# Writing the turned image from inside the chunk steps instead of between images (attention layer and selective scan, one Trainium2 core)

## The chip, the cores and the metric

The kernel runs on one core of a Trainium2 chip. A core has five engines with instruction streams of their own: TensorE (PE; its weight loads are listed apart as PEld), VectorE (DVE), ScalarE (ACT), GpSimd (POOL) and SyncE (SP), which here only issues transfers. Sixteen DMA engines move data between HBM and the on-chip memory (SBUF, 128 partitions); matrix products land in PSUM. An instruction waits for others through semaphores, and each engine takes its instructions in order. The metric is the device time of one execution in microseconds: 9565.71 us, the median of three runs of the kernel before.

## The reference

Two layers act on eight images of 128 x 128 pixels with 128 channels. Layer 0 is linear attention with a normalization. Layer 1 is a gated state-space layer with four scan directions. Cut to what matters for the change:

```python
xb, z = split(x @ Win)                      # 256 channels each
xb = silu(depthwise_conv3x3(xb) + conv_b)   # u
xf = xb.reshape(Bb, Cd, L)                  # rows first
xt = transpose(xb, (0, 1, 3, 2)).reshape(Bb, Cd, L)   # columns first: the turned image
xs = stack([xf, xf[..., ::-1], xt, xt[..., ::-1]])
x_dbl = einsum('bcl,cd->bdl', xs, Wxproj)   # 8 rows of dt, 1 of B, 1 of C
delta = softplus(dt_weight @ dt + dt_bias)
# scan: state = exp(delta*A)*state + delta*u*B ;  y = state*C + u*D
y = y0 + back(y1) + turn_back(y2) + turn_back(back(y3))
out = layernorm(y * silu(z)) @ Wout
```

The batch and the four directions are folded together in a way that mixes them: image `b` serves as direction `b // 2` for the outputs 0 to 3 (b even) or 4 to 7 (b odd). So the terms `u*D` of images 4, 6, 2 and 0 (and of 5, 7, 3 and 1) are summed into the same arrays.

## The kernel before

Three stages run one after another. `layer0` computes the attention and writes `x1` to HBM. `layer1_front` makes u from `x1` (projection, convolution, silu) and writes what the scans read: u times B in natural and in turned order (`ubs`), the ten rows of dt, B and C (`xds`, and split into three bfloat16 parts in both orders, `xps`), and the sums of u times D (`gts`, then `gs`). `layer1_scan` runs the scans and the output, behind a barrier of all engines (L722). The change lies in `layer1_front`.

**The front.** It goes through the images in the order of `SEQ` (4, 6, 5, 7, 0, 1, 2, 3). An image is 16 chunks of 1024 pixels (8 columns w of 128 h), and `step(n)` (L639) is one chunk: 128 steps, software pipelined from n-1 to n+2. Channels are two halves `c` of 128 partitions. The instruction order within each engine is exactly the program order (`in_order`).

In a step, TensorE projects (`project`, L475) and computes two of the nine convolution taps (`taps_pe`, L499). ScalarE copies the projection out of PSUM with the two edge columns that neighbouring chunks exchange (`place`, L483: L487, L491, L492), and computes three taps (`taps_act`, L513), which GpSimd adds up (L515). VectorE adds these to the PSUM sum (L521) and computes four taps (L523). ScalarE applies the silu (`silu`, L530) into `ures`, which holds the whole image. `rows` (L539) makes the ten rows, `keep_rows` (L544) stores them through two alternating buffers, `spread` (L551) spreads B over the partitions with the selector `bsel`, and `by_b` (L560) multiplies `ures` in place and stores it. `sum_d` (L579) scales u by D. Except for images 4 and 5, whose term is the first, the earlier sum is loaded (`load_sum`, L577; a gathering load, L575, for images 0 and 1), added by GpSimd (L595, or L592 for images 0 and 1) and stored again (`store_sum`, L600).

**The end of an image.** In the first step of the next image, `leave` (L626) is called in the midst of the step. It copies `ures` in turned order, in 32 pieces of 128 x 1024, into a staging buffer `turned` (L634: ScalarE for two in five, VectorE for the rest) and stores each (L635, 4096 contiguous bytes for each partition). Between them it loads the ten rows again with the columns on the partitions (L608), transposes them on TensorE (L616), splits both orders into bfloat16 parts on VectorE (`split3`, L44 and L46) and stores these (L624).

**What sets the order.** All transfers of the front are issued by SP, in program order, so a transfer whose data is late holds up all later ones. Staging buffers are rings: tag `tb` four buffers (taps, u times D, `turned`, parts), `ta`, `tc` and `d` two each. In the scan stage GpSimd issues transfers too: L855 adds `gs` onto `y` while it transfers.

Of the kernel before, what the change touches and what calls it, by code (L numbers as in the profile page):

```python
# [8 lines left out]
F32 = mybir.dt.float32  # L9
BF16 = mybir.dt.bfloat16  # L10
AF = mybir.ActivationFunctionType
# [5 lines left out]
P = 128  # L17
B = 8
# [4 lines left out]
R = 8  # L23
# [14 lines left out]
NAT, TURN = 0, 1  # L38


def split3(nc, parts, x):

    for j in range(3):
        nc.vector.tensor_copy(parts[j], x)  # L44
        if j < 2:
            nc.vector.tensor_tensor(x, x, parts[j], ALU.subtract)  # L46


def pipeline(n, stages):
# [334 lines left out]
def layer1_front(ctx: ExitStack, tc, x1, win, conv_w, conv_b, wxp, d_par, ubs, xds, xps, gts, gs):  # L384
# [25 lines left out]

    ident = const.tile([P, P], F32, name="ident1")
    make_identity(nc, ident)
    one3 = const.tile([3, P], BF16, name="one3")
    nc.vector.memset(one3, 1.0)
    cw = const.tile([P, NC2, 9], F32, name="cw")
    nc.sync.dma_start(cw, conv_w.rearrange("(c p) t -> p c t", p=P))
    cb = const.tile([P, NC2], F32, name="cb")
# [2 lines left out]
    wx = const.tile([P, NC2, 32], F32, name="wx")  # L420
    nc.vector.memset(wx, 0.0)
    nc.sync.dma_start(wx[:, :, 0 : R + 2], wxp.rearrange("(c p) r -> p c r", p=P))
    bsel = const.tile([P, 2, P], F32, name="bsel")
    for hf in range(2):
        nc.vector.tensor_copy(bsel[:, hf, :], ident[:, 32 * hf + R : 32 * hf + R + 1].to_broadcast([P, P]))
    sd = const.tile([P, K, NC2], F32, name="sd")
    nc.sync.dma_start(sd, d_par.rearrange("(k c p) o -> p k (c o)", p=P, c=NC2))
    wi = const.tile([P, NC2, P], F32, name="wi")
# [11 lines left out]
            nc.vector.tensor_tensor(wt[:, j, c, :], wi[:, c, :], p, ALU.mult)  # L440


    xins, xbs, xdt = [], [], []
    for i in range(2):
        xi = const.tile([P, CW + 1, H + 2], F32, name=f"xi{i}")
        nc.gpsimd.memset(xi, 0.0)
        xins.append(xi)
        xb = const.tile([P, NC2, CW + 2, H + 2], F32, name=f"xb{i}")
        nc.gpsimd.memset(xb, 0.0)
        xbs.append(xb)  # L450
        xd = const.tile([P, 512], F32, name=f"xd{i}")
        nc.gpsimd.memset(xd, 0.0)
        xdt.append(xd)
    ures = big.tile([P, NC2, L], F32, name="ures")
    uturn = ures.rearrange("p c (w h) -> p c h w", h=H)
    inner = slice(1, H + 1)
# [4 lines left out]
    def place_of(n):  # L461
        return SEQ[n // NCH % B], n % NCH
# [20 lines left out]
    def place(n, c):  # L483

        g = n % NCH
        xb, old = xbs[n % 2], xbs[(n - 1) % 2]
        nc.scalar.copy(xb[:, c, 1 : CW + 1, inner], pxs.pop((n, c)))  # L487
        if g == 0:
            nc.gpsimd.memset(xb[:, c, 0, :], 0.0)
        else:  # L490
            nc.scalar.copy(old[:, c, CW + 1, inner], xb[:, c, 1, inner])  # L491
            nc.scalar.copy(xb[:, c, 0, inner], old[:, c, CW, inner])  # L492
        if g == NCH - 1:
            nc.gpsimd.memset(xb[:, c, CW + 1, :], 0.0)

# [44 lines left out]

    def keep_rows(n):
        b, g = place_of(n)
        t = xdt[n % 2]
        nc.scalar.copy(t[0:64, :], prs.pop(n))  # L544
        for hf in range(2):
            s = slice(g * CH + hf * 512, g * CH + hf * 512 + 512)
            nc.sync.dma_start(xds[b][:, s], t[32 * hf : 32 * hf + R + 2, :])

    def spread(n, hf):
        pbs[n, hf] = p = pm.tile([P, 1, 512], F32, name="pb", tag="m")  # L550
        nc.tensor.matmul(p[:, 0, :], bsel[:, hf, :], xdt[n % 2], start=True, stop=True)  # L551

    def by_b(n):

# [14 lines left out]

    def load_sum(n, c):  # L570
        b, g = place_of(n)
        if b // 2 != 2:
            gls[n, c] = gl = wp.tile([P, CH], F32, name="gl", tag="d", bufs=2)
            if b // 2 == 0:
                nc.sync.dma_start(gl.rearrange("p (e q) -> p e q", e=NCH), gts[b % 2, c, :, :, g])  # L575
            else:
                nc.sync.dma_start(gl, sums_at(n, c))  # L577

    def sum_d(n):  # L579
        b, g = place_of(n)  # L580
        s = b // 2
        for c in range(NC2):
            t = wp.tile([P, CH], F32, name="du", tag="tb", bufs=4)
            u, dst = ures[:, c, g * CH : g * CH + CH], t
            if s >= 2:
                u = u.rearrange("p (w i h) -> p w i h", w=CW, h=8)
                dst = t.rearrange("p (i w h) -> p w i h", w=CW, h=8)
            nc.scalar.activation(dst, u, AF.Copy, scale=sd[:, s, c : c + 1])
            if s == 0:
                gl = gls.pop((n, c)).rearrange("p (e h) -> p h e", h=8)  # L590
                tw = t.rearrange("p (w h) -> p w h", w=CW)
                nc.gpsimd.tensor_tensor(tw, tw, gl, ALU.add)  # L592
            elif s != 2:
                gl = gls.pop((n, c))
                nc.gpsimd.tensor_tensor(gl, gl, t[:, ::-1] if s % 2 == 1 else t, ALU.add)  # L595
                t = gl
            dus[n, c] = t

    def store_sum(n, c):
        nc.sync.dma_start(sums_at(n, c), dus.pop((n, c)))  # L600

    half = (R + 2) // 2
    xws = {}

    def load_rows(b, i):
        r = slice(i * half, i * half + half)
        xws[b, i] = x = wp.tile([P, half, H], F32, name="xw", tag="d", bufs=2)
        nc.sync.dma_start(x, xds[b].rearrange("r (w h) -> w r h", h=H)[:, r, :])  # L608

    def split(b, i):  # L610

        r = slice(i * half, i * half + half)
        x = xws.pop((b, i))
        pt = pj.tile([P, half, P], F32, name="ptx", tag="pj")
        for j in range(half):
            nc.tensor.transpose(pt[:, j, :], x[:, j, :], ident)  # L616
        y = wp.tile([P, half, W], F32, name="xh", tag="tb", bufs=4)
        nc.scalar.copy(y, pt)
        for order, v in ((TURN, y), (NAT, x)):
            q = wp.tile([P, 3, half, P], BF16, name="parts", tag="tb", bufs=4)  # L620
            split3(nc, [q[:, j] for j in range(3)], v)
            dst = xps[b, order].rearrange("j r (a e) -> a j r e", e=P)
            for j in range(3):
                nc.sync.dma_start(dst[:, j, r, :], q[:, j])  # L624

    def leave(b):  # L626

        for i in range(2):
            load_rows(b, i)
        for k in range(NC2 * NCH):  # L630
            c, i = divmod(k, NCH)
            t = wp.tile([P, CW, W], F32, name="turned", tag="tc" if k % 3 == 2 else "tb", bufs=2 if k % 3 == 2 else 4)
            copy = nc.scalar.copy if k % 5 in (1, 3) else nc.vector.tensor_copy
            copy(t, uturn[:, c, i * CW : i * CW + CW, :])  # L634
            nc.sync.dma_start(ubs[b, TURN][c][:, i * CH : i * CH + CH], t.rearrange("p h w -> p (h w)"))  # L635
            if k % 10 == 9 and k < 20:
                split(b, k // 10)

    def step(n):  # L639

        live, then, later, before = 0 <= n < N, 0 <= n + 1 < N, 0 <= n + 2 < N, 1 <= n <= N
        b, g = place_of(n)
        if live:
            taps_dve(n, 0)
        if before:
            keep_rows(n - 1)
        if then:
            project(n + 1, 1)
            place(n + 1, 1)
        if live:  # L650
            taps_pe(n, 1)
        if later:
            load(n + 2)
        if before:
            for c in range(NC2):
                store_sum(n - 1, c)
        if live and g != 0:
            for c in range(NC2):
                load_sum(n, c)
        if before:  # L660
            for hf in range(2):
                spread(n - 1, hf)
        if before and g == 0:
            by_b(n - 1)
            leave(place_of(n - 1)[0])
        if live and g == 0:
            for c in range(NC2):
                load_sum(n, c)
        if then:
            taps_act(n + 1, 0)  # L670
        if live:
            silu(n, 0)
        if then:
            taps_pe(n + 1, 0)
        if later:
            project(n + 2, 0)
        if live:
            taps_dve(n, 1)
        if then:
            taps_act(n + 1, 1)  # L680
        if before and g != 0:
            by_b(n - 1)
        if live:
            silu(n, 1)
        if later:
            place(n + 2, 0)
        if live:
            rows(n)
            sum_d(n)

    with in_order(tc):
        for n in range(-2, N + 1):
            step(n)


@with_exitstack
def layer1_scan(ctx: ExitStack, tc, ubs, xps, zs, gs, dtw, dtb, a_log, gamma, beta, w_out, out):
# [36 lines left out]
    for dst, src, rows in ((wparts, dtw.rearrange("k r d -> r k d"), R), (bparts, dtb.rearrange("o (k d) -> o k d", d=D2), 1)):  # L734
        x = wp.tile([rows, K, D2], F32, name="w32", tag="sp", bufs=2)
        nc.sync.dma_start(x, src)
        q = wp.tile([rows, 3, K, D2], BF16, name="w16", tag="ub", bufs=4)
        split3(nc, [q[:, j] for j in range(3)], x)
        for j in range(3):
            if rows == 1:  # L740
                nc.sync.dma_start(dst[j : j + 1], q[:, j])
            else:
                nc.sync.dma_start(dst[j], q[:, j])
# [466 lines left out]
```

## Time and profile before

| what | value |
|---|---|
| median of three runs | 9565.71 us (9555.7 to 9566.26) |
| profiled execution: span of the core | 9556.3 us |
| front: first L521 to last copy of L634 | 2377.7 to 4825.1 us |
| one chunk step in the front (start of L521 to the same in the next step) | 15.26 us |
| start of an image to the start of the next | 304.6 to 306.9 us; 16 steps alone are 244.2 us |
| VectorE busy over the span | 8129.7 us (85%) |
| GpSimd busy over the span | 7192.2 us (75%) |

The span runs from the first to the last instruction of one profiled execution; the runs are timed apart. Its slices show all three stages at once; the front's own windows are read below. In lines of groups, the number after the count is the busy time in us, then the mean duration of one in ns, then the engine's idle time before them with what ended it. In windows, each engine has its busy time and its number of instructions, and the last columns are TensorE's granted clock, the busy share of the DMA engines and GB/s.

### The profile page before, as it was taken

Reading aid. Unit: us, or ns where it says so; the run is one execution under the profiler, and the core shown is the slowest. Engines: PE = TensorE matmul, PEld = TensorE weight load, DVE = VectorE, ACT = ScalarE, POOL = GpSimd, SP = SyncE. Lnnn points to the kernel's source line nnn. Section 1 sums busy time; section 2 is a strip of 40 time slices with the busy share of each in tenths; the row PEclk is TensorE's granted clock in tenths of the full one; section 3 lists DMA queues with packets and bytes.
Section 4 is the critical chain, followed back from the end, with each engine's and each line's share of the span. In section 5 each row is a group of like instructions: output and inputs, shape, how many; then the busy total and the mean of one; then the engine's idle time right before and its main releaser. Section 6 shows DMA issues by size and latency. Waiting matters only on the chain. (4 is left out here: it accounts for less than half of the span.)

```text
span 9556.3 us, 89734 instructions
## 1 busy us (share of the span) xinstructions
PE 6281.6 (66%) x24190; PEld 3101.4 (32%) x24352; DVE 8129.7 (85%) x8188; ACT 7202.0 (75%) x8288; POOL 7192.2 (75%) x4361
## 2 busy tenths in 40 slices
PE   8999999898977788777823544636345363543636
PEld 5556655554322233222300311404123040220403
DVE  6667765564988889888979999999999999999996
ACT  5556555567877788777878788888888888888884
POOL 3445544455665578776859999999999999999997
PEclk9999999999988899888955665757557585665857
DMA  2332233313476678987765957759487685867858
GB/s 91 135 133 81 95 133 132 133 71 140 172 266 232 229 262 247 266 263 269 243 204 165 257 174 207 240 174 269 154 228 219 186 260 165 244 190 198 245 165 212
DMA packets 1034807, 1851.21 MB, mean 194 GB/s; under 512 B 274852, under 2 KB 500772, under 8 KB 1026112
## 3 DMA queue, kind: packets, MB, share of 16 engines
q1 hardware_dynamic: 999488, 1711.23, 54.2%
q0 software_dynamic: 34816, 134.23, 7.3%
q8 instruction: 199, 3.26, 0.1%
q14 instruction: 304, 2.49, 0.1%
HBM read 1153.03 MB, written 692.12 MB: 193 GB/s over the span
## 5 line engine op out<-in xcount | busy, mean ns | idle before, releaser
L893 POOL TENSOR_TENSOR ubt<-ubt,sp 128x1024 f32<-128x1024 f32 x1024 | 2457.9, 2458 | 161.0 <-ACT sp L886 74.3
L882 PE MATMUL px<-rows,dtw 128*128 128x512 bf16 x1893 | 909.5, 573 | 2271.7 <-DVE y L943 1063.5
L515 POOL TENSOR_TENSOR tap<-tap 128x1024 f32<-128x1024 f32 x512 | 1206.1, 2367 | 640.1 <-ACT tap L513 517.9
L523 DVE SCALAR_TENSOR_TENSOR acc<-xb,cw,acc 128x1024 f32<-128x1024 f32 x1024 | 1320.6, 1290 | 52.7 <-ACT tap L513 0.9
L886 ACT ACTIVATE sp<-px 128x1024 f32<-128x1024 f32 x1024 | 1046.0, 1024 | 420.7 <-PE px L882 265.6
L951 POOL TENSOR_TENSOR y<-y,ubt 128x512 f32<-128x512 f32 x768 | 1160.0, 1557 | 142.9 <-DVE ubt L924 141.9
L505 PE MATMUL acc<-xi,wt 128*128 128x512 f32 x2048 | 952.2, 608 | 383.9 <-ACT ures L530 383.6
L903 DVE TENSOR_TENSOR_SCAN ubt<-px,ubt 128x1024 f32<-128x1024 f32 x512 | 1177.0, 2332 | 25.9 <-POOL ubt L893 19.2
L901 DVE TENSOR_TENSOR_SCAN ubt<-px,ubt 128x1024 f32<-128x1024 f32 x512 | 1178.3, 2332 | 14.1 <-POOL ubt L893 6.3
L882 PEld LDWEIGHTS <-dtw 128*128 128x128 bf16 x2048 | 163.9, 109 | 3066.2 <-issue 865.9
L890 ACT ACTIVATE px<-sp,sa 128x1024 f32<-128x1024 f32 x1024 | 1110.2, 1109 | 6.1
L513 ACT ACTIVATE tap<-xb,cw 128x1024 f32<-128x1024 f32 x768 | 834.0, 1139 | 68.1 <-POOL tap L515 67.8
L282 POOL TENSOR_TENSOR q<-q,qs 128x512 f32<-128x512 f32 x256 | 271.2, 1060 | 691.5 <-DVE qs L281 691.5
L886 ACT ACT_TABLE_LOAD x512 | 656.9, 1283 | 164.5 <-PE px L882 129.2
L505 PEld LDWEIGHTS acc<-xi,wt 128*128 128x128 f32 x2048 | 383.6, 192 | 928.3 <-ACT ures L530 486.1
L890 ACT ACT_TABLE_LOAD x512 | 656.9, 1283 | 9.2
L1016 PEld LDWEIGHTS px<-wg,z 128*128 128x128 f32 x4096 | 553.8, 218 | 118.6 <-issue 113.5
L909 PE MATMUL pc<-rows,csel 128*128 128x512 bf16 x1017 | 512.7, 585 | 88.9 <-DVE rstd L1004 79.9
L1016 PE MATMUL px<-wg,z 128*128 128x128 f32 x4096 | 554.1, 301 | 0.0
L478 PE MATMUL pxb<-xi,wi 128*128 128x512 f32 x1024 | 495.9, 606 | 4.3 <-ACT xb L487 4.3
L943 DVE TENSOR_TENSOR y<-y,px 128x1024 f32<-128x1024 f32 x384 | 468.7, 1221 | 14.7 <-DVE px L931 0.5
L298 ACT ACTIVATE sq<-o 128x512 f32<-128x512 f32 x256 | 161.2, 630 | 418.2 <-DVE o L296 416.9
(155 smaller groups left out, 15187.7 us busy)
## 6 DMA issues: line engine op xcount, KB each, us to landing
ubt<-ubs SPq DMA_DIRECT2D x512, 1024.0 KB
zs<-z SPq DMA_DIRECT2D x512, 256.0 KB
ubs<-ures SPq DMA_DIRECT2D x256, 512.0 KB
ubs<-turned SPq DMA_DIRECT2D x256, 512.0 KB
z<-zs SPq DMA_DIRECT2D x256, 512.0 KB
y<-gs POOLq DMA_DIRECT2D x128, 1024.0 KB, 10.5
rows<-xps SPq DMA_DIRECT2D x1536, 60.0 KB
xi<-x SPq DMA_DIRECT2D x120, 576.0 KB
```

What stands on the lines that cost most here:

```text
L505: nc.tensor.matmul(acc[:, s, :], wt[:, j, c, :], x, start=(j == 0), stop=(j == len(ON_PE) - 1))
L513: nc.scalar.activation(t, at(n, c, *d), AF.Copy, scale=cw[:, c, tap(*d) : tap(*d) + 1])
L515: nc.gpsimd.tensor_tensor(sums[n, c], sums[n, c], t, ALU.add)
L523: nc.vector.scalar_tensor_tensor(acc, at(n, c, *d), cw[:, c, tap(*d) : tap(*d) + 1], acc, ALU.mult, ALU.add)
L882: nc.tensor.matmul(p[:, hf * 512 : hf * 512 + 512], sl.dw[:, c * P : c * P + P], src, start=True, stop=True)
L886: nc.scalar.activation(t, da[n, c], AF.Softplus)
L890: nc.scalar.activation(da[n, c], sp[n, c], AF.Exp, scale=sa[:, sl.s, c : c + 1])
L893: nc.gpsimd.tensor_tensor(ubt[n][:, c, :], ubt[n][:, c, :], sp.pop((n, c)), ALU.mult)
L901: nc.vector.tensor_tensor_scan(e[:, ::-1], x[:, ::-1], e[:, ::-1], start, ALU.mult, ALU.add)
L903: nc.vector.tensor_tensor_scan(e, x, e, start, ALU.mult, ALU.add)
L951: nc.gpsimd.tensor_tensor(v[:, c], v[:, c], h[:, c], ALU.add)
L1016: nc.tensor.matmul(po[:, w, :], z[:, c, w * H : w * H + H], wg[:, c, :], start=(c == 0), stop=(c == NC2 - 1))
```

## The change

- `leave` goes. The turned copies stay 32 for each image, but each now covers 16 rows h by 64 columns w of a half image, and two are made in each step (`turn`), eight steps behind: one after the first four taps of VectorE, one at the end of the step. `copy_on` names the engine: both on GpSimd in the steps of images 4 and 5; VectorE and GpSimd in those of 6, 7, 2 and 3; VectorE and ScalarE in those of 0 and 1. That is 96 on VectorE, 113 on GpSimd, 32 on ScalarE. The last 15 are made after the last step (`tail`).
- Each copy is stored in runs of 64 elements (256 bytes) at a pitch of 512 bytes (`store_turned`), where it was 4096 contiguous bytes before.
- The rows' split is cut into five pieces of two rows, spread over ten steps of the next image (`split_step`), on VectorE in the steps of images 0 and 1, else on GpSimd. The last image's is done in `tail`.
- For images 6, 7, 2 and 3 the earlier sum is no longer loaded and added: ScalarE writes u times D (reversed) into the ring `d`, and GpSimd issues a transfer that adds it onto the sum in HBM (`add_sum`).
- `place` makes one edge copy of two columns instead of two copies. The row buffer `xd` is single instead of double, and `bsel` is replaced by a broadcast column of the identity.

```diff
@@ layer1_front
-    one3 = const.tile([3, P], BF16, name="one3")
-    nc.vector.memset(one3, 1.0)
-    bsel = const.tile([P, 2, P], F32, name="bsel")
-    for hf in range(2):
-        nc.vector.tensor_copy(bsel[:, hf, :], ident[:, 32 * hf + R : 32 * hf + R + 1].to_broadcast([P, P]))
...
+    both = const.tile([P, NC2, 2, CW + 2, H + 2], F32, name="xb")
...
+    edges = [
+        (edge[:, :, 2 * CW + 3 :: -(2 * CW + 3), 1 : H + 1], edge[:, :, 1 : 2 * CW + 3 : 2 * CW + 1, 1 : H + 1]),
+        (edge[:, :, CW + 1 : CW + 3, 1 : H + 1], edge[:, :, CW + 3 : CW - 1 : -3, 1 : H + 1]),
+    ]
@@ place
-            nc.scalar.copy(old[:, c, CW + 1, inner], xb[:, c, 1, inner])
-            nc.scalar.copy(xb[:, c, 0, inner], old[:, c, CW, inner])
+            dst, src = edges[n % 2]
+            nc.scalar.copy(dst[:, c], src[:, c])
@@ sum_d
-            elif s != 2:
-                gl = gls.pop((n, c))
-                nc.gpsimd.tensor_tensor(gl, gl, t[:, ::-1] if s % 2 == 1 else t, ALU.add)
-                t = gl
...
+            dus[n, c] = t = wp.tile([P, CH], F32, name="du", tag="d", bufs=2)
+            dst = t[:, ::-1] if s % 2 == 1 else t
+            if s >= 2:
+                u = u.rearrange("p (w i h) -> p w i h", w=CW, h=8)
+                dst = dst.rearrange("p (i w h) -> p w i h", w=CW, h=8)
+            nc.scalar.activation(dst, u, AF.Copy, scale=sd[:, s, c : c + 1])
...
+    def add_sum(n):
+        s = place_of(n)[0] // 2
+        if s % 2 == 1:
+            for c in range(NC2):
+                nc.gpsimd.dma_start(sums_at(n, c), dus.pop((n, c)), accum_op=ALU.add)
+
+    HALF = W // 2
+    COPIES = NC2 * NCH // 2
+    turned = {}
+
+    def turn(k, copy, tag, bufs):
+        m, r = divmod(k, COPIES)
+        b, hf = SEQ[m // 2], m % 2
+        c, i = divmod(r, COPIES // NC2)
+        turned[k] = t = wp.tile([P, 2 * 8, HALF], F32, name="turned", tag=tag, bufs=bufs)
+        copy(t, uturn[:, c, 16 * i : 16 * i + 16, hf * HALF : hf * HALF + HALF])
+
+    def store_turned(k):
...
+        dst = ubs[b, TURN][c].rearrange("p (h w) -> p h w", w=W)
+        nc.sync.dma_start(dst[:, 16 * i : 16 * i + 16, hf * HALF : hf * HALF + HALF], turned.pop(k))
+
+    def copy_on(n, second):
+        s = place_of(n)[0] // 2 if n < N else 2
+        if s == 0:
+            return nc.scalar.copy if second else nc.vector.tensor_copy
+        if s % 2 == 1 and not second:
+            return nc.vector.tensor_copy
+        return nc.gpsimd.tensor_copy
...
+    def split_step(n):
+
+        q, d = divmod(n - 2, NCH)
+        q -= 1
+        j, odd = divmod(d, 2)
+        if not 0 <= q < B or n >= N or d > NROW:
+            return
+        eng = nc.vector if place_of(n)[0] // 2 == 0 else nc.gpsimd
+        if odd:
+            turn_rows(q, 2 * j, 2, "sy", 1)
+            split(q, 2 * j, 2, NAT, eng, "sq", 1)
+        else:
+            if j:
+                split(q, 2 * j - 2, 2, TURN, eng, "sq", 1)
+            if 2 * j < NROW:
+                load_rows(q, 2 * j, 2, "sx", 1)
@@ step(n), in program order
+        ka, kb = 2 * (n - 8) - 1, 2 * (n - 8)
         if live:
             taps_dve(n, 0)
+        if ka >= 0:
+            turn(ka, copy_on(n, False), "tc", 2)
+        if before:
+            add_sum(n - 1)
         if before:
             keep_rows(n - 1)
...
             load(n + 2)
+        store_parts()
         if before:
-            for c in range(NC2):
-                store_sum(n - 1, c)
+            store_sum(n - 1)
...
+        if ka - 1 >= 0:
+            store_turned(ka - 1)
...
-        if before and g == 0:
-            by_b(n - 1)
-            leave(place_of(n - 1)[0])
...
-        if before and g != 0:
+        if before:
             by_b(n - 1)
+        if ka >= 0:
+            store_turned(ka)
...
             rows(n)
             sum_d(n)
+        if kb >= 0:
+            turn(kb, copy_on(n, True), "tc", 2)
+        split_step(n)
+
+    def tail():
+        store_parts()
+        q, k0 = B - 1, 2 * (N - 8)
+        store_turned(k0)
+        for i in range(2):
+            load_rows(q, 5 * i, 5, "d", 2)
+        for k in range(k0 + 1, 2 * B * COPIES):
+            i = k - k0 - 1
+            copy = (nc.vector.tensor_copy, nc.scalar.copy, nc.gpsimd.tensor_copy)[i % 3]
+            turn(k, copy, "tc" if i % 3 == 2 else "tb", 2 if i % 3 == 2 else 4)
+            store_turned(k)
+        for i in range(2):
+            turn_rows(q, 5 * i, 5, "tb", 4)
+            for order in (TURN, NAT):
+                split(q, 5 * i, 5, order, nc.vector, "tb", 4)
+                store_parts()
```

## The prediction

> **What bounds the kernel now.** I read the page's busy shares first, then the front by windows, one for each kind of stretch: steps of image 5 (no earlier sum to load), of image 0 (a gathering load), of image 2 (a plain load), and the end of an image.
>
> ```profile
> span 9556.3 us, 89734 instructions
> PE 6281.6 (66%) x24190; PEld 3101.4 (32%) x24352; DVE 8129.7 (85%) x8188; ACT 7202.0 (75%) x8288; POOL 7192.2 (75%) x4361
> ```
>
> ```profile
> core 0: us, PE busy (x) PEld busy (x) DVE busy (x) ACT busy (x) POOL busy (x), PEclk, DMA share, GB/s
> ...
> 3005.00:3233.00 228.00, 215.20 (x540) 82.55 (x538) 219.66 (x178) 206.73 (x251) 141.44 (x65) 1.00 0.50 175
> ...
> 3618.00:3838.00 220.00, 206.22 (x517) 79.24 (x516) 211.51 (x172) 199.53 (x243) 216.79 (x92) 1.00 0.89 241
> ...
> 4230.00:4458.00 228.00, 215.19 (x540) 82.64 (x540) 219.65 (x178) 204.96 (x251) 212.01 (x95) 1.00 0.72 242
> 2632.00:2684.00 52.00, 2.63 (x10) 1.86 (x10) 30.90 (x40) 24.32 (x14) 0.00 (x0) 0.53 0.97 358
> ```
>
> In the steps VectorE is busy 96% (219.66 of 228): it sets the 15.26 us. Image 0 is near three limits at once: VectorE 96%, GpSimd 99%, DMA 89%. At the end of an image (last row) the convolution stands still, GpSimd does nothing, and DMA is 97% busy. The line of the copies says so too:
>
> ```profile
> L634 DVE COPY turned<-ures x152: 1014/1025/1035, 2631.9 to 4821.9; 128x1024 f32<-128x1024 f32 x152
> L634 ACT COPY turned<-ures x104: 1913/1922/1981, 2631.9 to 4823.2; 128x1024 f32<-128x1024 f32 x104
>   DMA ubs<-turned: 225.8, 117
> ```
>
> Front = 128 steps x 15.26 = 1953 us, and 499 us for eight ends (seven of about 62, the last about 65), in all the 2452 us from 2377.7 to about 4830. Only the 499 can be won; all that moves into the steps must find room there.
>
> **What the Trainium skill says.** "GPSIMD Engine Reference", section 7 (performance pitfalls): reading SBUF with a step over 8 bytes costs about 2.9 cycles an element instead of 1.9. The trace has no GpSimd copy, but its strided adds agree: L592, with one strided input, takes 2.87 us where the plain L595 takes 2.36. "SBUF — State Buffer", section "SBUF: two separate sides": VectorE operations in a two-port mode or with two SBUF inputs share a locked port pair with GpSimd, and the loser blocks. The trace agrees for VectorE:
>
> ```profile
> L971 DVE TENSOR_TENSOR z<-y,z x120: 1214/1690/4032, 5377.8 to 9539.8; 128x1024 f32<-128x1024 f32 x120
> ```
>
> beside a busy GpSimd, half take 1.69 us or more against 1.21; and the two L425 copies of 128x128, begun as GpSimd's memsets ran, took 6.67 us each. "DMA: Bandwidth & Descriptors", section "Specifications": transfers below 512 bytes are not at line rate. In the trace a packet of 4096 bytes takes 163 ns (25 bytes/ns), one of 256 bytes 16.7 ns when written (`xps`, in the image ends; 15 bytes/ns) and 23.4 ns when read at a wide pitch (the gathering load in image 0's steps).
>
> **The change part by part.**
>
> Removed: the eight ends, 499 us. What of them comes back:
>
> VectorE, images 6, 7, 2, 3, 0, 1: one copy a step, 1.02 us (L634). The lock wait isn't shown for it: at least 0, at most a GpSimd add, 2.37 (L515). L971's median loss is 0.47, the L425 case says more; I take 1.0. Step by VectorE: 15.26 + 1.02 + 1.0 = 17.3. The copy also stands ahead of `by_b` and the second half's taps, so it is on the path.
>
> GpSimd: four tap adds, 4 x 2.37 = 9.5 a step. A copy isn't shown: at least 0.9 (the rate of L449's memset, 2.26 us for 2600 elements), at most 2.9 (L592's price; the skill's 2.9 cycles give an estimate of 2.5 at its 1.2 GHz). I take 2.2. A split is five operations on 256 elements: two subtractions at 0.66 (add rate of L515) plus three casts at 0.35 (about half that), 2.4 us, on ten of sixteen steps; bounds 1.5 to 4. An adding transfer's issue is shown by L855:
>
> ```profile
> L855 POOL DMA_DIRECT2D y<-gs x128: 1180/1251/1756, 5265.2 to 9508.8; - x128
> DMA to landing us min/median/max: 8.4/10.5/13.8
> ```
>
> two a step are 2.5 us; the adds it replaces (L595) were 4.7. So: images 6, 7, 2, 3: 9.5 + 2.2 + 2.5 + 2.4 + 1.0 (blocked by VectorE's copy) = 17.6 in split steps, 15.2 else; image 5: 9.5 + 4.4 + 2.4 = 16.3 or 13.9; image 4 has no split and stays under 15.26. Behind `add_sum` in GpSimd's queue stand the next tap adds, for which VectorE's L521 waits. The ring `d` has two buffers: ScalarE's next u times D waits for the landing; issued some 3 us into the step plus 8 to 10 us to land (half L855's bytes) is inside a step, just.
>
> Images 0 and 1: the split runs on VectorE: 2 x 0.42 + 3 x 0.29 (L46 and L44 scaled from 640 to 256 elements with 0.15 us fixed) = 1.7, with 0.4 of lock wait on each of the five (near L971's 0.47), 3.7 in all. Step: 17.3 + 3.7 = 21.0 in split steps. ScalarE takes a copy of 1.92 (L634): 13.85 busy a step + 1.92 - 0.4 (edge copies) = 15.4, covered.
>
> DMA, time a step on 16 engines: image 5 now 0.51 x 15.26 = 7.8; image 2 0.737 x 15.26 = 11.2; image 0 0.896 x 15.26 = 13.7. Added: two turned stores of 2048 packets, 2 x 2048 x 16.7 ns / 16 = 4.3; splits 0.65 (their 7680 packets of 256 bytes and the rows' loads, over 16 steps). An adding transfer of 128 packets at 341 ns (those of L855) is 2.7, two are 5.4, against 6.1 for two loads and two stores at 190 ns. Image 5: 12.7; images 6, 7, 2, 3: 15.5; images 0, 1: 18.7, or 19.2 at the 97% that the ends reach: no longer hidden. The price of a 256-byte write at a 512-byte pitch isn't shown: from 15 (fastest seen) to twice 16.7.
>
> At nothing: the single `xd` (its readers, two small stores and two matmuls early in a step, have the rest of it; a late landing would hold ScalarE's L544 and then the taps); the row transposes (PE 94% busy at 15.26, 0.5 us more, covered by the longer step); `bsel` (L425, under GpSimd's memsets and the first load); SP's extra issues, queued behind the x load. `store_parts` waits on SP for GpSimd's split, with stores behind it that nobody awaits soon.
>
> Steps by the largest of the three: image 4: 16 x 15.26 = 244. 6, 7, 2, 3: 10 x 17.6 + 6 x 17.3 = 280 each, 1119. 5: 10 x 16.3 + 6 x 15.3 = 255. 0, 1: 10 x 21.0 + 6 x 19.2 = 325 each, 650. Tail: 17 stores x 2.14 + splits 8.0 + rows 2.3 = 46.7 us of DMA, 48 at 97%, after some 7 us of the last step: 55. Sum 2323 against 2452: 129 us less. Profile 9556 - 129 = 9427; the median of the runs stands 10 us above the span, so 9437.
>
> **The rivals.**
>
> A, the cover holds: lock waits near zero, GpSimd copies near 1.5. Steps 16.3 (VectorE alone) for 6, 7, 2, 3; 15.6 for 5; 18.4 for 0, 1 (the gathering load at 20 ns a packet, nearer its fastest 18). 244 + 1043 + 250 + 589 + 55 = 2181: 271 less, 9295. For: L971's shortest show no wait. Against: L425.
>
> B, GpSimd becomes the bound: copy 2.9, split 4, lock 1.0. Split steps 9.5 + 2.9 + 2.5 + 4.0 + 1.0 = 19.9, else 17.3: 303 each; image 5 (19.3, 15.3) 285; 0 and 1 as above 325. 244 + 1212 + 285 + 650 + 55 = 2446: 6 less, about 9560. With two of the three high bounds it is about 9520. For: strided adds are dear. Against: one input, not two.
>
> C, slower: the half-row packets cost twice 16.7, 33 ns. Turned stores are then 8.5 a step. Image 5 needs 17.3 at 97%, 6, 7, 2, 3 20.3, 0 and 1 23.6; 4 17.3 in its second half. 261 + 1299 + 277 + 755 + 92 = 2684: 232 more, 9798. It decides from about 26 ns a packet on, where the gain is gone. For: the gathering load's 23.4. Against: `xps` writes at 16.7.
>
> **How the numbers follow.** Likeliest (9437; its own range 9340 to 9510) 0.48; A 0.22; B 0.17; C 0.08; other stalls that cost more 0.05. The kernel's measurement tells 0.2%, 19 us, from no change. Faster: 0.48 + 0.22 + two thirds of B, 0.82; same 0.05, the middle of B; slower 0.13, C, the rest of B and the stalls. The range, 9245 to 9555, takes in A and most of B and leaves out C.
>
> **What would show it.** No stretch of some 50 us with GpSimd idle; starts of L521 at 15.3 (image 4), about 17.5 (6, 7, 2, 3), 16 (5) and 20 (0, 1); VectorE copies near 2 us beside a busy GpSimd (near 1.0 would be A); GpSimd copies of 2.2; 256-byte packets under 20 ns (over 26 is C). Waits of ScalarE's u times D for a landing on `gs` or `gts` would mean that the ring is the limit, which the sum prices at nothing. The prediction is wrong if the steps of 0 and 1 stay below 17 or those of the other images exceed 19.

## The result, and the profile after

The changed kernel takes 9507.75 us (median of 6 runs, 9504.55 to 9544.83); the kernel before, run beside it, 9560.14 (6 runs, 9546.26 to 9566.26). The ratio is 0.9957, interval 0.9944 to 0.997: faster, by 52 us where 129 were forecast. The profiled execution is the longest of the six, so its spans add up to some 37 us more than those of a median run; the same kernel run again, further down, has the same stages.

The page, busy time by engine:

```profile
span 9543.0 us, 89342 instructions
...
PE 6385.5 (67%) x24190; PEld 3126.7 (33%) x24352; DVE 8152.7 (85%) x8094; ACT 7056.8 (74%) x8002; POOL 7383.7 (77%) x4727
```

The busy shares hardly moved. The front did: in the profile its first L521 starts at 2374.6 us and the first instruction of the scan stage at 4816.6, so it takes 2442 us, against 2454 before by the same two marks; the scan stage after it is as long as it was (4726 us against 4724.5). The length of an image, from its first L521 to the next image's first:

| image, in order | 4 | 6 | 5 | 7 | 0 | 1 | 2 | 3 | tail |
|---|---|---|---|---|---|---|---|---|---|
| before | 244.7 | 304.6 | 306.3 | 305.5 | 306.4 | 306.9 | 306.0 | ~306 | 66 (last end) |
| forecast | 244 | 280 | 255 | 280 | 325 | 325 | 280 | 280 | 55 |
| after | 244.5 | 295.6 | 253.7 | 292.8 | 352.5 | 353.4 | 289.4 | ~290 | ~70 |

Images 4 and 5 came as forecast. Images 6, 7, 2 and 3 take 49 us too much together, 0 and 1 take 56, the tail 15: 120 us, which is the difference between the forecast span of 9427 and 9543 but for 4. The stages by windows, for images 5, 7, 0 and the tail (the columns as in the prediction's table):

```profile
2914.00:3168.00 254.00, 233.03 (x594) 89.47 (x594) 238.78 (x193) 220.19 (x244) 238.23 (x153) 1.00 0.83 249
3168.00:3461.00 293.00, 243.97 (x585) 90.29 (x580) 258.50 (x209) 219.05 (x243) 242.23 (x167) 0.95 0.90 216
3461.00:3813.00 352.00, 264.70 (x591) 100.73 (x591) 328.25 (x259) 250.71 (x259) 240.80 (x103) 0.88 0.87 225
4748.00:4816.00 68.00, 6.21 (x20) 2.63 (x16) 21.00 (x27) 11.69 (x9) 15.19 (x9) 0.55 0.91 226
```

In image 7 no engine is full: VectorE is busy 258.5 us of 293 and GpSimd 242, and DMA is at 90%. In image 0 VectorE is busy 328 of 352 us, where the forecast had 314 for it, waits included (10 x 21.0 + 6 x 17.3); GpSimd does nothing for 111 us. So something stretches VectorE in image 0, and something is late in image 7.

**Image 0.** The groups of its window show what is stretched (busy us, mean ns of one, then idle time before them):

```profile
L617 DVE COPY turned<-ures 128x1024 f32<-128x1024 f32 x16 | 38.2, 2390 | 7.5 <-DMA ubs<-turned 7.5
L44 DVE CAST parts<-xw 128x256 bf16<-128x256 f32 x15 | 18.1, 1209 | 0.3
L44 DVE CAST parts<-xh 128x256 bf16<-128x256 f32 x15 | 17.7, 1182 | 0.3
L46 DVE TENSOR_TENSOR xw<-xw,parts 128x256 f32<-128x256 f32 x10 | 14.7, 1466 | 7.5 <-PE ptx L647 7.2
```

A copy was 1.02 us before; a cast of this size was taken at 0.29 plus 0.4. The timeline of the same image (start, length, engine, work; lines of other engines are left out) shows it in single instructions:

```profile
3595.99 4.77 POOL L515 TENSOR_TENSOR tap<-tap 128x1024 f32<-128x1024 f32 x2 [4.38 <-ACT tap L513]
3598.97 2.69 DVE L617 COPY turned<-ures 128x1024 f32<-128x1024 f32 x1
...
3611.11 0.29 DVE L44 CAST parts<-xh 128x256 bf16<-128x256 f32 x1
...
3611.84 5.75 POOL L586 TENSOR_TENSOR du<-du,gl 128x1024 f32<-128x1024 f32 x2 [1.88 <-ACT du L583]
3611.90 2.98 DVE L44 CAST parts<-xh 128x256 bf16<-128x256 f32 x1
```

The same cast takes 0.29 us when GpSimd stands still and 2.98 when it begins 0.06 after an add of about 2.9: it ends with that add. The copy begins 0.55 after GpSimd's second tap add and takes the rest of it and 0.9 more. (In a timeline line with x2, the length is that of both adds together.)

**Image 7.** The groups of its window:

```profile
L478 PE MATMUL pxb<-xi,wi 128*128 128x512 f32 x127 | 70.9, 686 | 32.6 <-DMA xi<-x 32.6
L617 POOL COPY turned<-ures 128x1024 f32<-128x1024 f32 x16 | 31.7, 1981 | 12.9 <-DMA ubs<-turned 12.9
L605 POOL DMA_DIRECT2D gts<-du x30 | 29.7, 1158 | 4.3 <-ACT du L593 2.5 <-issue 0.8 <-DVE acc L523 0.2
L617 DVE COPY turned<-ures 128x1024 f32<-128x1024 f32 x16 | 20.7, 1292 | 5.7 <-DMA ubs<-turned 5.7
L44 POOL CAST parts<-xh 128x256 bf16<-128x256 f32 x15 | 6.0, 400 | 0.6
```

The VectorE copy takes 1.29 on average, its median 1.07: hardly any lock here. New is that TensorE waits for the load of `x`, the image itself (first row), 32.6 us here and 131 over the front, all but a few of them in images 6, 7, 2 and 3. The timeline of one such step:

```profile
3241.41 2.61 POOL L605 DMA_DIRECT2D gts<-du  x2
3244.00 0.38 SPq L471 DMA_DIRECT2D xi<-x  x1
...
3254.35 3.54 PE L478 MATMUL pxb<-xi,wi 128*128 128x512 f32 x4 [4.19 <-DMA xi<-x]
```

GpSimd issues both adding transfers, SP issues the load right behind them, and TensorE gets the load 10 us later, having stood for 4.19.

### The profile page after: what moved, and what is told of

Read it like the earlier page. It is cut to its first block, busy times and chain, and to the rows that moved or that the text cites. A ratio compares the mean times of both kernels' runs of the same rounds, so it can differ in the third digit from the quotient of the medians.

```text
span 9543.0 us, 89342 instructions
## 1 busy us (share of the span) xinstructions
PE 6385.5 (67%) x24190; PEld 3126.7 (33%) x24352; DVE 8152.7 (85%) x8094; ACT 7056.8 (74%) x8002; POOL 7383.7 (77%) x4727
## 5 line engine op out<-in xcount | busy, mean ns | idle before, releaser
L971 DVE TENSOR_TENSOR_SCAN ubt<-px,ubt 128x1024 f32<-128x1024 f32 x512 | 1176.6, 2331 | 25.8 <-POOL ubt L961 19.6
L505 PE MATMUL acc<-xi,wt 128*128 128x512 f32 x2048 | 988.3, 627 | 196.5 <-ACT ures L530 196.1
L478 PE MATMUL pxb<-xi,wi 128*128 128x512 f32 x1024 | 536.4, 649 | 135.6 <-DMA xi<-x 131.3
```

Source lines behind the costliest of these rows:

```text
L505: nc.tensor.matmul(acc[:, s, :], wt[:, j, c, :], x, start=(j == 0), stop=(j == len(ON_PE) - 1))
L971: nc.vector.tensor_tensor_scan(e, x, e, start, ALU.mult, ALU.add)
```

## The experiments

Two theories came out of this. **Lock**: in images 0 and 1 VectorE's copies and splits wait for GpSimd's adds. Its rival: ScalarE, which got the second copy (L617, 1.92), or GpSimd's own work sets the step there. **Collision**: in images 6, 7, 2 and 3 the two adding transfers, issued just ahead of the load of `x`, make it late. Its rival: DMA is simply full there, whatever the order ("load").

### The changed kernel once more

No edit.

> The changed kernel itself, once more, to see how far its stretches repeat. Its first profile had the eight images at 244.5 (image 4), 295.6 (6), 253.7 (5), 292.8 (7), 352.5 (0), 353.4 (1), 289.4 (2), 290.5 us (3), and that execution was one of its slowest. If the spread of its runs (9505 to 9545 us) comes from the front, this profile shows images 6, 7, 2, 3 some 5 to 10 us shorter each when the time is near 9507; if from the scan stage, the images stay as they were.

Measured: 9526.53 (13 runs, 9488.72 to 9549.74), ratio 0.9961 (0.9949 to 0.9973). Images 244.6, 292.2, 253.9, 297.8, 350.7, 351.6, 290.9, 288; waits for `x` of 33 to 41 us in each of 6, 7, 2 and 3. The stages are those of the first profile, but the runs spread over 61 us.

### Images 0 and 1: the split on GpSimd

```diff
-        eng = nc.vector if place_of(n)[0] // 2 == 0 else nc.gpsimd
+        eng = nc.gpsimd
```

> The changed kernel with the rows' split of images 7 and 0 (made in the steps of images 0 and 1) on GpSimd, as everywhere else. Theory 'lock': in images 0 and 1 VectorE is blocked by GpSimd, and the five operations a step of the split pay 3 to 4 us for it; without them the split steps fall from 24.4 us in the mean to about 20, images 0 and 1 from 353 to about 320 each, and the kernel to about 9445. Rival 'DMA': images 0 and 1 stand at what the DMA engines can do (18.7 us a step of packets, at 0.87 busy); moving the split changes no packet, so they stay at 345 to 353 and the kernel at 9500 to 9508.

Measured: 9424.4 (4 runs, 9401.59 to 9464.31), ratio 0.9876 (0.9854 to 0.9899): 102 us under the changed kernel of the same series. Images 0 and 1 are 308.0 and 302.1. Image 0 by windows:

```profile
3444.00:3751.00 307.00, 248.79 (x590) 94.04 (x590) 262.35 (x208) 250.74 (x259) 271.36 (x153) 0.94 1.00 257
```

VectorE's busy time fell by 66 us, GpSimd's rose by 31. DMA is at 1.00 and VectorE waits 37.1 us for stored pieces, so DMA now sets the step. The 45 and 51 us that images 0 and 1 lost came with the split, as the lock has it. Both rivals fall: ScalarE still has its copy, and GpSimd has more work than before. Of VectorE's 66 us, 55 are the split's own operations; most of the rest is the copy, which GpSimd's adds now meet less often (1.61 us on average instead of 2.39). Image 6 came out at 270.8 in this profile and 2 at 272.1 with the same code as before, 7 and 3 at 300.2 and 280: how often the load of `x` is late varies from one execution to the next, and so does part of the gain here.

### Images 0 and 1: GpSimd's add left out

```diff
                 tw = t.rearrange("p (w h) -> p w h", w=CW)
-                nc.gpsimd.tensor_tensor(tw, tw, gl, ALU.add)
                 continue
```

> The changed kernel without GpSimd's adds of the earlier sum in images 0 and 1 (the sums lack the images before; the loads stay, no packet changes). GpSimd isn't the limit there (15.3 of 22 to 26 us), so only what it does to others can show. Theory 'lock': the casts and subtractions of the split, which take 1.2 and 0.9 us in the mean with single ones at 2.98, fall to 0.29 and 0.43, and images 0 and 1 from 352 to 305-325 each. Rival 'own work': VectorE is full with its own operations and waits for TensorE's transposes; images 0 and 1 stay at 340 or more.

Measured (one run): 9442.13; images 0 and 1 303.8 and 304.3. The groups of image 0:

```profile
L44 DVE CAST parts<-xw 128x256 bf16<-128x256 f32 x15 | 8.5, 566 | 0.3
L44 DVE CAST parts<-xh 128x256 bf16<-128x256 f32 x15 | 6.3, 421 | 0.3
L46 DVE TENSOR_TENSOR xw<-xw,parts 128x256 f32<-128x256 f32 x10 | 4.3, 426 | 3.9 <-PE ptx L646 3.7
```

The same VectorE instructions, in the same places, take 0.57, 0.42 and 0.43 us instead of 1.21, 1.18 and 1.47, once GpSimd's L586 is gone. The copy falls too, from 2.39 on average to 1.42. This shows the lock in the instructions themselves. It is one run, and taking the add out also takes 5.7 us a step off GpSimd; that this alone is not the gain is shown by the run before, in which GpSimd had more to do. The program puts L586 (`sum_d`) and the split (`split_step`) next to each other at the end of a step, so they meet every time.

### Images 0 and 1: both copies on ScalarE

```diff
         if s == 0:
-            return nc.scalar.copy if second else nc.vector.tensor_copy
+            return nc.scalar.copy
```

> The changed kernel with the turned copies of images 0 and 1 all on ScalarE, none on VectorE; the split stays on VectorE. Theory 'lock': the VectorE copy there takes 2.34 us in the mean, of which 1.3 are waiting for GpSimd's tap adds; without it these steps lose 2 us each, images 0 and 1 fall from 352 to about 320, the kernel by 60 to 70 us. Rival 'ScalarE': two copies of 2.0 us bring ScalarE to 17.4 us a step with its work coming later; images 0 and 1 stay within 15 us of 352.

Measured: 9525.39 (20 runs, 9490.42 to 9567.65), ratio 0.9973 (0.9961 to 0.9984); images 0 and 1 356.3 and 357.6, no gain. My expectation was wrong. VectorE had 38 us less to do, and yet steps of 17.0 and of 28 to 30 alternate. The timeline of image 0 shows the splits still blocked, one after the other:

```profile
3575.54 5.74 POOL L586 TENSOR_TENSOR du<-du,gl 128x1024 f32<-128x1024 f32 x2 [2.19 <-ACT du L583]
3575.63 2.93 DVE L44 CAST parts<-xw 128x256 bf16<-128x256 f32 x1
3578.60 2.96 DVE L46 TENSOR_TENSOR xw<-xw,parts 128x256 f32<-128x256 f32 x1
3581.59 0.29 DVE L44 CAST parts<-xw 128x256 bf16<-128x256 f32 x1
```

Taking the copy away leaves the splits where they meet L586. In the ten split steps image 0 does gain some 13 us in all. In the other six, where VectorE has neither split nor copy, the steps take up to 23.2 us instead of at most 19.5, some 17 in all, and the gain is lost. So the rival holds as well: ScalarE, which has one copy already, can't take a second for nothing. The first combination below shows this by itself.

### Images 6, 7, 2, 3: the adding transfers left out

```diff
             for c in range(NC2):
-                nc.gpsimd.dma_start(sums_at(n, c), dus.pop((n, c)), accum_op=ALU.add)
+                dus.pop((n, c))
```

> The changed kernel without the adding transfers of images 6, 7, 2 and 3 (the sums of u times D lack these images). Theory 'DMA': those images are long because the load of x lands late behind the adding transfers, which move for 391 ns a packet and 6 us a step; without them TensorE's wait for x goes and the images fall from 292 to 265-270 each, the kernel to about 9410. Rival 'GpSimd and lock': only the 2.2 us of issuing on GpSimd go; the steps stay over 17 us, images at 280 or more, the kernel at 9460 or more.

Measured: 9433.12 (9426.5 to 9440.16), ratio 0.9872 (0.9857 to 0.9887). Images 6, 7, 2 and 3: 268.4, 264.4, 265.2, 267.6; no wait for `x` at all; images 0 and 1 as they were (348, 353). The runs spread over 14 us instead of 61. So the waits come with these transfers; both theories allow that.

### Images 6, 7, 2, 3: the turned stores in one piece a partition

The same bytes are stored, as 4096 contiguous ones per partition instead of sixteen half rows of 256.

```diff
-        nc.sync.dma_start(dst[:, 16 * i : 16 * i + 16, hf * HALF : hf * HALF + HALF], turned.pop(k))
+        at = (8 * hf + i) * CH
+        nc.sync.dma_start(ubs[b, TURN][c][:, at : at + CH], turned.pop(k).rearrange("p h w -> p (h w)"))
```

> The changed kernel with each turned piece stored as 4096 contiguous bytes for each partition (at its piece's place, so the turned image in HBM is in another order than the scan expects). Theory 'DMA load': 1.7 us a step less of DMA work (two stores at 1.3 instead of 2.14); where DMA limits, images 6, 7, 2, 3 lose 10 to 20 us each and the kernel comes to 9430-9465. Rival 'collision with the adding transfers only': the x load stays late, these images lose under 5 us each, the kernel stays over 9485. In both, images 0 and 1 stay at 345 or more if VectorE limits them.

Measured: 9462.82 (9455.44 to 9476.68), ratio 0.9904 (0.989 to 0.9919). Images 6, 7, 2 and 3: 269.8, 289.5, 286.6, 279. DMA is busy only 0.80 to 0.84 there, and TensorE still waits 10, 36, 33 and 22 us for `x`. The kernel's time is what "load" forecast (9430 to 9465). But a DMA that is a sixth idle on average isn't full, and the wait is still there: as the cause of the wait, "load" is unlikely. The half rows do cost something: 64 us against the changed kernel of the same series, some 44 of them in these four images.

### Images 6, 7, 2, 3: the old adding

Loads, GpSimd's adds and stores as before the change, for images 6, 7, 2 and 3, with u times D back in the ring `tb`; the rest of the change stays.

```diff
-        if b // 2 == 0:
+        if b // 2 != 2:
...
+                nc.sync.dma_start(gl, sums_at(n, c))
...
+                nc.gpsimd.tensor_tensor(gl, gl, t[:, ::-1], ALU.add)
...
-        if s % 2 == 0:
+        if True:
...
-        if before:
-            add_sum(n - 1)
```

> The changed kernel with the earlier sums of images 6, 7, 2 and 3 loaded, added by GpSimd and stored again, as in the kernel before, instead of the adding transfers. The DMA time stays about the same (6.1 instead of 6.2 us a step), but these transfers stand behind the x load in SP's queue. GpSimd has 4.7 us of adds for 2.2 us of issuing: 19 us in split steps, 16.6 else. Theory 'collision': x is no longer late, GpSimd's sum is the limit, images 6, 7, 2, 3 at 285 to 295 each, so the kernel within 30 us of the changed one. Rival 'load': x stays late and GpSimd's work comes on top: images at 305 or more, the kernel over 9560.

Measured: 9602.21 (9589.12 to 9610.98), ratio 1.0045 (1.003 to 1.006): slower than the kernel before. Images 308.5, 307.8, 304.9, 308. The waits of image 7 from its third step on (who waits for which transfer: us in total, times, longest):

```profile
DVE turned L625 <- DMA ubs<-turned: 37.4, 13, 4.4
...
PE pxb L478 <- DMA xi<-x: 10.6, 8, 2.8
```

The time is outside what "collision" forecast and is the rival's number, but not for the rival's reason: the load of `x` is less late now, and VectorE waits for the turned stores instead. Why these are late was not tried. Against the 9526.53 of the changed kernel in the series above this is 76 us more (the kernel before is the same in both within 1 us): the adding transfers, for all their waits, are a gain.

### Images 6, 7, 2, 3: both adding transfers later

```diff
-        if before:
-            add_sum(n - 1)
...
             taps_act(n + 1, 0)
+        if before:
+            add_sum(n - 1)
```

> The changed kernel with only the place of the adding transfers moved in GpSimd's queue: behind the first half's two tap adds instead of ahead of them, about 5 us later, when the x load (issued 2 us after the early adding transfers) has mostly landed. No byte, packet or instruction changes. Theory 'collision': the early adding transfers share the DMA engines with the x load and make it late; issued later they don't, TensorE's wait for x shrinks to under a third of its 131 us, images 6, 7, 2, 3 fall from about 292 to 265-275 each, the kernel by 70 to 100 us against the changed kernel (9507 to 9527), to about 9430. Rival 'load': these images stand at the sum of their packets (0.90 busy); the order within a step makes little difference, under 25 us in all, 9490 or more; or the later landing makes ScalarE's next u times D wait and it gets slower.

Measured: 9622.9 (9619.34 to 9631.44), ratio 1.0069 (1.0054 to 1.0084): slower; images 305.6, 306.5, 303.9, 309.6. The waits of image 7:

```profile
DVE turned L617 <- DMA ubs<-turned: 45.2, 14, 4.2
...
ACT du L593 <- DMA gts<-du: 43.9, 19, 3.7
```

The forecast of "collision" (9430) failed, although no wait for `x` stands in the list any more: the time of issue does decide that. But the pair is now issued some 16 us after the step's first L521, about 10 later than before, and lands too late for the ring `d` (two buffers), so ScalarE waits at L593. VectorE's copy waits 45.2 us for the turned stores, whose ring `tc` has two buffers, where it waited 5.7 before. One wait is gone and two others have come.

### Images 6, 7, 2, 3: one early, one late

```diff
-            add_sum(n - 1)
+            add_sum(n - 1, 0)
...
             taps_act(n + 1, 0)
+        if before:
+            add_sum(n - 1, 1)
```

> The changed kernel with the two adding transfers of a step apart: the first channel half's where it was, the second's behind the first two tap adds. Theory 'collision': x waits behind one adding transfer (2.7 us) instead of two, TensorE's wait for x falls from about 35 us an image (6, 7, 2, 3) to under 15, and the second lands early enough that ScalarE's u times D hardly waits (in the run with both late: 44 us an image); images at 268-280, the kernel at 9440 to 9480. Rival 'rings': the later transfer again holds the ring of u times D or the turned stores; images at 290 or more, 9510 or more.

Measured: 9470.65 (9465.83 to 9474.69), ratio 0.9907 (0.9892 to 0.9922). Images 268.9, 274.8, 270.3, 271.2, with DMA at 0.97 to 0.98. The waits of image 7:

```profile
DVE turned L617 <- DMA ubs<-turned: 8.9, 6, 2.1
ACT du L593 <- DMA gts<-du: 8.7, 6, 2.7
PE pxb L478 <- DMA xi<-x: 3.8, 5, 1.7
```

(`add_sum` takes the channel half now.) The same bytes in the same packets, 6 to 9 us apart in most steps instead of at once: 33 us of waiting for `x` become 4, the images lose 18 to 27 us each, and the spread falls to 9. DMA is busier than before and the wait is gone: this separates collision from load.

### Put together

All of them have the split on GpSimd. The first has both copies of images 0 and 1 on ScalarE and both adding transfers late.

> The changed kernel with three edits: the split always on GpSimd, the copies of images 0 and 1 on ScalarE, the adding transfers behind the first two tap adds. If 'lock' and 'collision' are the two causes, images 0 and 1 stand at their DMA work (about 300 each, as with the split alone on GpSimd, or a little less), images 6, 7, 2, 3 at 265-275, image 5 at 254, image 4 at 244: the front ends some 190 us earlier than in the changed kernel, the kernel at 9325 to 9360. If only the first holds, 9400 to 9430.

Measured: 9629.05 (9615.89 to 9633.17), ratio 1.0072 (1.0057 to 1.0087); images 6, 7, 2, 3 at 306 to 310 as with the late transfers alone, 0 and 1 at 366.6 and 349.2. The forecast (9325 to 9360) failed. Image 1 issues no adding transfers in its steps, and against the run with the split alone on GpSimd (302.1) only ScalarE's second copy is new there. Its waits:

```profile
DVE acc L521 <- PE acc L505: 107.0, 32, 6.0
ACT turned L617 <- DMA ubs<-turned: 19.7, 15, 2.9
```

VectorE is busy 240 us of 349 and waits for TensorE, which waits in turn for ScalarE's silu. ScalarE makes its second copy at the end of a step, waits there for a buffer, and only then begins the next step. So two copies on ScalarE cost image 1 47 us, without any split on VectorE.

The second issues the adding transfers of a step in the step itself, right behind `sum_d`:

```diff
-        if before:
-            add_sum(n - 1)
...
             sum_d(n)
+            add_sum(n)
```

> The split always on GpSimd, and both adding transfers issued as soon as u times D is there, ahead of GpSimd's turned copy and split, 2 to 4 us earlier than before. Theory 'collision': more of their 5.4 us is done when x is issued; TensorE's wait for x falls to under 20 us an image, images 6, 7, 2, 3 at 265-278, images 0 and 1 at about 305, the kernel at 9370 to 9410, against 9424 with the split alone. Rival: GpSimd waits for ScalarE's u times D in front of its copy and split, and its tap adds come later: no gain, 9420 or more.

Measured: 9383.28 (9377.23 to 9392.68), ratio 0.9817 (0.9802 to 0.9831). Images 6, 7, 2 and 3 take 270 to 275, 0 and 1 309 and 307. The waits for `x` are still 23 to 25 us an image, where under 20 were expected. Their sum is not their cost: here nearly every step of image 7 waits, 1 to 2.7 us, and the steps take some 16.9; in the changed kernel steps of 16.2 have waits up to 2.5 as well, and most steps of 20 us and more are those with 3 to 6 us of it. In this run the second of the pair is always issued 3.1 to 4.2 us ahead of the load of image 7. In the changed kernel that distance varies from step to step; where it was under 2 us, TensorE stood for up to 4.5 us, where it was over 3, mostly for 1 to 2.5.

The third sets the adding transfers apart:

> Both: the split always on GpSimd, and the two adding transfers apart. If the causes add up: images 0 and 1 at about 305, 6, 7, 2, 3 at 268-280, the kernel at 9360 to 9400. If the later transfer holds a ring, 9425 or more.

Measured: 9376.22 (9373.17 to 9383.0), ratio 0.9807 (0.9791 to 0.9824): 183 us under the kernel before in the same series, and 130 to 150 under the two medians of the changed one. Images 6, 7, 2 and 3 take 268 to 276. Image 0 by windows:

```profile
3420.00:3730.00 310.00, 250.34 (x582) 94.31 (x578) 259.70 (x208) 249.15 (x257) 272.90 (x153) 0.93 0.99 255
```

DMA is at 0.99 there and at 0.95 to 0.97 in 6, 7, 2 and 3. This version is the fastest found. In images 0 and 1 the DMA limits it (VectorE waits 43.4 us for turned stores in image 0); in 6, 7, 2 and 3 the DMA and VectorE's own step of 16.2 are both near their limit, and which of them holds it was not tried.

## Why the prediction came half true

The sign and the range held; the size did not. By its own steps:

- **The removed ends, images 4 and 5**: right. 244.5 and 253.7 against 244 and 255, and the split steps of image 5 take 16.2 where GpSimd's sum said 16.3; a stretch with GpSimd idle no longer exists except in the tail.
- **Half rows** (rival C): the 256-byte packets average 16.4 ns in image 5 and 17.1 in image 7; 16.7 was taken. C is excluded. The run with contiguous stores shows that the half rows aren't free either (64 us), where the sum had their DMA time as hidden in most images.
- **GpSimd's prices** (rival B): the copy 1.98 (2.2 taken), the cast 0.40 (0.35), the subtraction 0.67 by the median (0.66), the issue of an adding transfer 1.1 on average (1.25). "GPSIMD Engine Reference", section 7, has 2.9 cycles an element, which gave an estimate of 2.5; the trace has 1.98, so the measurement decides. GpSimd idles 111 us in image 0: B's mechanism is false, although its 9560 lies nearer to the measured 9508 than my 9437.
- **The failed step, images 0 and 1: "with 0.4 of lock wait on each of the five (near L971's 0.47), 3.7 in all".** I priced the wait by L971's median loss, an average over times when GpSimd happens to be there and not. In this place it is always there. The split took about 5.5 us a split step, its blocked operations up to 2.98 each, and the copy 2.7 or 3.1 there instead of 2.0. VectorE's step is then 15.26 + 2.9 + 5.5 + about 0.7 of waits for TensorE's row transposes (7.2 us an image on L46, unpriced) = 24.4, as measured on average over a pair. With GpSimd's add gone, or the split on GpSimd, some 45 us an image or more went. What is left then is the forecast's own DMA limit: 308.0 and 302.1 are 19.3 and 18.9 us a step, against 19.2. The case at hand, L425 under the memsets, I used for the copy alone and not for the split, where it was the better guide; I also misread it, for its two records overlap, and the pair took 6.77 us together. "SBUF — State Buffer", section "SBUF: two separate sides", says that whichever starts first has the shared ports for its whole instruction and the other blocks: the trace agrees (the 2.98 cast ends with the add).
- **The same step in images 6, 7, 2 and 3: "I take 1.0"**: wrong the other way. By the median the copy loses 0.05 there (1.07), and quiet steps are 16.2, 15.26 + 1.02, as rival A had it. In ten of the sixteen steps of image 7 GpSimd issues an adding transfer while the copy runs; nine of these copies take 1.05 to 1.28 us. The tenth takes 4.21 and ends 0.9 after a tap add that began 0.3 behind it, which the order of starting doesn't explain. Where those are left out, the copy mostly starts together with a tap add and it is the add that loses, 3.3 us instead of 2.36.
- **The failed step of these images: DMA as a sum, and nothing for the load of `x`.** "15.5" a step, under 17.3, was to be hidden. It measured 16.4 (the adding packets average 382 to 397 ns there, 341 taken), near the engines' 16.2, and that alone leaves about 262 us an image. The rest, up to 296, is not load but order: the load of `x`, which TensorE awaits some 6 us after its issue, comes behind two transfers of 512 KB whose issue began 1 to 4.5 us earlier. Of this load the prediction had only "SP's extra issues, queued behind the x load", at nothing. I looked for a late landing at the ring `d` alone ("would mean that the ring is the limit"); there is none to speak of until the transfers are moved. I priced the adding transfers' issue on GpSimd and their bytes, and never asked what the load issued right behind them would meet. That 280 an image is no further from 290 to 296 is partly luck: the lock wait and GpSimd's sum made the steps 17.3 to 17.6 where the engines need 16.2, and the missing wait took up that difference and more.
- **The tail: 70 for 55.** DMA does 62 us of work in its window at 0.91, 46.7 taken: the turned and split packets and row loads are 50.4, and 11.3 are the last step's adding transfers (6.0) and other stores (5.3), which I left out; then the last splits (L663) wait for the stores ahead of them on SP.
- **At nothing**: the single `xd`, the edge copy (now 0.41 instead of two of 0.30) and `bsel` show next to no wait in the trace (TensorE waits some 5 us for `xd` over the whole front), but were not tried by themselves.

Left open: how the adding transfers delay the load. "DMA: Bandwidth & Descriptors", section "Queues, rings and completion order", says that an engine takes turns between its queues a packet at a time, a packet being there a group of descriptors. In the trace `x` moves in records of 512 bytes in one queue (29 ns on average in image 7) and the adding transfers in records of 4096 bytes in another (391 ns), so turns of this kind would hold up `x`. How many records make one turn isn't shown, and no run here separates this from other causes; what the runs show is that the wait comes and goes with the time of issue.

## What to carry to other kernels

Price a lock between VectorE and GpSimd by what stands next to the instruction in the order of the program, not by a mean over the kernel: if both come at the same point of every step, each operation of a small group can pay the rest of a long GpSimd one, as the split did here, and the group is worth trying on GpSimd. For DMA ask two questions, not one: does the sum of the packets fit the step, and what was issued just ahead of the one transfer that somebody awaits soon. If a pair of large transfers stands there, issue them apart, and check that each still lands before its ring comes round.

## What was not expected of the hardware

- Which of the two pays for the lock turns on little more than a tenth of a microsecond. Where VectorE's copy and a tap add begin within 0.01 us of each other (images 6 and 7), the copy takes 1.06 and the add 3.3. With the add 0.13 to 0.16 ahead (image 0), the copy takes 3.1 and the add 2.34; with the add 0.55 ahead, 2.69 and 2.35.
- A 4096-byte adding packet takes 327 ns with little traffic beside it and, on average, some 380 to 405 in a loaded step; a plain one of the same size averages 160 to 178.
- Half rows of 256 bytes at a pitch of 512 in HBM cost about what other 256-byte writes do: with few other packets among them, 16.4 ns on average in image 5 (median 15), against 16.7 before in the image ends; in the loaded steps of images 6, 7, 2 and 3 it is 17 (median 18).
- The pair of adding transfers close ahead of the load makes the time of a run uncertain as well. The shortest and the longest lie 61 us apart with it, and 63 in four runs with the split on GpSimd; with the transfers apart, issued in the step itself or left out, 9 to 15 in four runs each. With contiguous stores the spread is 21 although the pair is there, so the pair alone doesn't make it.
